# Group norm, attention and projection on one core: how the first chunks of x are loaded and normalised

## The chip, the cores and the metric

One core of a Trainium2 chip runs the whole kernel. The metric is the device time of one execution in microseconds, lower is better. The time before is 1604.12 us, the median of three runs (1601.0 to 1604.14).

## The reference

An attention layer over images. x has 4 images of 512 channels by 48 x 48 = 2304 positions, in float32. Cut to what matters:

```python
xr = x.reshape(b, 32, c // 32, h, w)
mean = xr.mean(axis=(2, 3, 4), keepdims=True)
var = xr.var(axis=(2, 3, 4), keepdims=True)
hn = ((xr - mean) * rsqrt(var + 1e-5)).reshape(b, c, h, w) * scale + bias
qkv = einsum('oc,bchw->bohw', qkv_w, hn) + qkv_b      # then to float16, 8 heads of 64
w = softmax(einsum('bhct,bhcs->bhts', q * s, k * s))
a = einsum('bhts,bhcs->bhct', w, v)
out = x + einsum('oc,bchw->bohw', proj_w, a) + proj_b
```

The normalisation takes one mean and one variance for each group of 16 channels over all positions. As scale and bias of a channel it is x * ga + gb, with rstd = (var + eps)^-0.5, ga = rstd * scale and gb = bias - mean * ga.

## The kernel before, in words

Channels lie on the 128 partitions, so an image is four chunks c of 128 channels, and each chunk is five pieces (blocks) j along the positions: four of 512 and a short one of 256 (`QBLOCKS`). A piece is one tile `hn[b, c, j]`, normalised in place.

The fast path has a prologue for image 0, and then one long stream in which scores, exponentials, values and the projections of later and earlier images are interleaved by a planner (`fill`, `put` and the lists of pieces with their costs and due times). The change touches the prologue alone. What sets its order is the order in which the program is written, since every engine takes its own instructions in order:

- `load_x` (L503) issues the pieces of x. Chunk 0 goes over two DMA queues in turn, pieces 0, 2 and 4 on SP and 1 and 3 on ACT (L537); then ACT issues the weights of k and of q for the first pair of heads (`load_w`), and all other pieces and weights go over SP. A tile's users wait for its load by one of eight DMA semaphores that are taken in turn, so a DMA also waits until the one eight places before it has landed.
- `keep_busy` (L1315) issues filler matmuls on TensorE, 16 ahead of everything and 4 after the first group's small products.
- `stats` and `aggregate` (L617 to L626) take mean and variance of each channel on VectorE: one statistics instruction a piece, then one aggregate into `moments`.
- `first_group` (L670) does chunk 0: the group means come from a tiny product with the matrix `share` (L678), the spread between a group's channels is added to the variance on VectorE (L679, L680), a second tiny product averages that (L681), POOL takes the power -0.5 (L686), and VectorE forms ga and gb (L690, L691).
- `group_scale` and `coefficients` (L632, L652) do the same for chunks 1 to 3 without TensorE: VectorE transposes `moments` in 32 x 32 squares, aggregates over the 16 channels of a group, POOL takes the power, and VectorE spreads the result back to channels. Between the two stand one or two statistics instructions of the next chunk, which fill VectorE while POOL works.
- `norm_chunk` (L701) normalises the five blocks of a chunk on ScalarE with scale ga and bias gb.
- Eight accumulation chains (k for all five blocks, q for the first three) stand in eight PSUM banks at once. The loop over c at the end (L1342) gives each chain the products of chunk c with the first pair's weights (`qk_steps`, L748), one block after another: k of blocks 0, 1, 2, 3, 4, then q of blocks 0, 1, 2. A block of 512 is two pairs of matmuls. TensorE meets each chunk for the first time in the order of those blocks.

After the last chunk the q chains for blocks 3 and 4 and the v chains follow, and then the stream begins.

Of the kernel before, what the change touches and what calls it, by code (L numbers as in the profile page):

```python
# [12 lines left out]
F32 = mybir.dt.float32  # L13
# [3 lines left out]
AF = mybir.ActivationFunctionType  # L17
ALU = mybir.AluOpType
# [6 lines left out]
GROUP = C // 32  # L25
EPS = 1e-5
P = 128
NC = C // P
# [14 lines left out]
QB = 512  # L43
QBLOCKS = [(o, min(QB, T - o)) for o in range(0, T, QB)]
NQ = len(QBLOCKS)
# [422 lines left out]
def fast_path(  # L468
# [12 lines left out]
    nc = tc.nc  # L481
# [11 lines left out]
    ps_s = ctx.enter_context(tc.tile_pool(name="ps_s", bufs=3, space=PSUM))  # L493
    ps_av = ctx.enter_context(tc.tile_pool(name="ps_av", bufs=1, space=PSUM))
# [3 lines left out]
    hn = {}  # L498
# [1 line left out]

    SPARE = {(1, 2): lambda c: ("res", RES), (1, 3): lambda c: (f"a32_{c}", 1)}

    def load_x(b, j, c, engine):  # L503

        o, n = QBLOCKS[j]
        name = f"x_{b}_{c}_{j}"
        if (b, j) in SPARE:
            tag, bufs = SPARE[b, j](c)
            t = work.tile([P, n], F32, tag=tag, bufs=bufs, name=name)
        else:  # L510
            t = xpool.tile([P, n], F32, tag=f"x{c}_{j}", name=name)
        engine.dma_start(t, x[b, bass.ts(c, P), o : o + n])
        hn[b, c, j] = t

    def load_block(b, j):
# [3 lines left out]
    gsc = const.tile([P, NC], F32, name="gsc")  # L519
    gbi = const.tile([P, NC], F32, name="gbi")  # L520
# [13 lines left out]

    for c in range(NC):
        for j in range(NQ):
            load_x(0, j, c, nc.scalar if c == 0 and j % 2 else nc.sync)  # L537
        if c == 0:
            load_w(1, slice(0, P), nc.scalar)
            load_w(0, slice(0, P), nc.scalar)  # L540
# [29 lines left out]
    mhalf = const.tile([P, 2], F32, name="mhalf")  # L570
# [31 lines left out]
    def small_bank(name):  # L602
        return ps_w.tile([P, QB], F32, tag="pw", name=name)


    stat, coef, ab = {}, {}, {}
# [5 lines left out]
    SQ = 32  # L612
    NGROUP = SQ // GROUP
    moments = const.tile([P, 3, SQ], F32, name="moments")
    nc.gpsimd.memset(moments, 1.0)

    def stats(b, j, c):  # L617

        if b not in stat:
            stat[b] = small.tile([P, NC, NQ, 6], F32, tag="st", bufs=1, name=f"st_{b}")  # L620
        nc.vector.bn_stats(stat[b][:, c, j, :], hn[b, c, j])  # L621

    def aggregate(b, chunks=ALL):
        for c in chunks:
            nc.vector.bn_aggr(
                moments[:, 1:, c], stat[b][:, c].rearrange("p j s -> p (j s)")  # L626
            )

    def small_tile(n, tag):
        return small.tile([P, n], F32, tag=tag, bufs=1, name=tag)  # L630
# [21 lines left out]
    def coefficients(b, chunks=ALL):  # L652
        both, spread, rstd = coef.pop((b, chunks[0]))
        nc.vector.tensor_copy(
            spread[:, 1], rstd.unsqueeze(2).to_broadcast((P, NGROUP, GROUP))
        )
        cols = small_tile(SQ * 2, "cols").rearrange("p (s c) -> p s c", s=2)
        nc.vector.transpose(cols, both)
        cs = slice(chunks[0], chunks[-1] + 1)
        ga, mga, gb = (  # L660
            small.tile([P, NC], F32, tag=f"{n}{chunks[0] % 2}", name=f"{n}_{b}")[:, cs]
            for n in ("ga", "mga", "gb")
        )
        nc.vector.tensor_tensor(ga, cols[:, 1, cs], gsc[:, cs], ALU.mult)
        nc.vector.tensor_tensor(mga, cols[:, 0, cs], ga, ALU.mult)
        nc.vector.tensor_tensor(gb, gbi[:, cs], mga, ALU.subtract)
        for i, c in enumerate(chunks):
            ab[b, c] = ga[:, i : i + 1], gb[:, i : i + 1]

    def first_group():  # L670

        mean, var = moments[:, 1, 0:1], moments[:, 2, 0:1]
        by = share.rearrange("p g j -> p (g j)")
        pm = small_bank("first_group")
        dev, var2, mg, veps, rstd = (
            small_tile(1, f"first_{n}") for n in ("dev", "var2", "mg", "veps", "rstd")
        )
        nc.tensor.matmul(pm[:, 0:1], by, mean, start=True, stop=True)  # L678
        nc.vector.tensor_tensor(dev, mean, pm[:, 0:1], ALU.subtract)  # L679
        nc.vector.tensor_scalar(var2, dev, dev, var, ALU.mult, ALU.add)  # L680
        nc.tensor.matmul(pm[:, 1:2], by, var2, start=True, stop=True)  # L681
        nc.vector.scalar_tensor_tensor(
            mg, pm[:, 0:1], -1.0, gsc[:, 0:1], ALU.mult, ALU.mult
        )
        nc.vector.tensor_scalar(veps, pm[:, 1:2], EPS, None, ALU.add)
        nc.gpsimd.tensor_tensor(rstd, veps, mhalf[:, 0:1], ALU.pow)  # L686

        def finish():
            ga, gb = small_tile(1, "first_ga"), small_tile(1, "first_gb")
            nc.vector.tensor_tensor(ga, rstd, gsc[:, 0:1], ALU.mult)  # L690
            nc.vector.tensor_scalar(gb, rstd, mg, gbi[:, 0:1], ALU.mult, ALU.add)  # L691
            ab[0, 0] = ga, gb

        return finish

    def norm(b, j, c):
        t = hn[b, c, j]
        ga, gb = ab[b, c]
        nc.vector.tensor_scalar(t, t, ga, gb, ALU.mult, ALU.add)

    def norm_chunk(b, c):  # L701

        ga, gb = ab[b, c]
        for j in range(NQ):
            t = hn[b, c, j]
            nc.scalar.activation(t, t, AF.Identity, bias=gb, scale=ga)

    def piece(us, run, first=False, last=False, when=None):
        return [us, run, first, last, when, 0, NG]
# [262 lines left out]
    av, acc, pts, avx, sums, rowd, ibs = {}, {}, {}, {}, {}, {}, {}  # L976

    stream = []
    for g in range(NG):
        for j, (o, n) in enumerate(QBLOCKS):  # L980
            count = NT * n // QB // BURST
# [255 lines left out]
    for b in range(B):  # L1237
        g = b * NPAIR
# [71 lines left out]

    busy = ppool.tile([P, 2, QB], F16, tag="p", name="busy")
    nc.vector.memset(busy[:, 0, :], 1.0)
    idle = ps_av.tile([P, QB], F32, tag="av", name="idle")

    def keep_busy(count):  # L1315
        for _ in range(count):
            nc.tensor.matmul(
                idle, busy[:, 0, :P], busy[:, 0, :], start=True, stop=True
            )

    def all_stats(c):
        for j in range(NQ):
            stats(0, j, c)
        aggregate(0, (c,))

    keep_busy(16)
    all_stats(0)
    first_coefficients = first_group()
    keep_busy(4)

    eight = [(1, j) for j in range(NQ)] + [(0, j) for j in range(8 - NQ)]
    banks = [
        t[:, i, :]
        for k in range(3)
# [5 lines left out]
    chains = [qk_steps(0, *a, bank) for a, bank in zip(eight, banks)]  # L1340

    for c in range(NC):  # L1342

        for j in range(NQ):
            if j == (1 if c < 2 else 2):
                if c == 0:
                    first_coefficients()
                else:
                    coefficients(0, (c,))
                norm_chunk(0, c)  # L1350
            if c + 1 < NC:
                stats(0, j, c + 1)
        if c + 1 < NC:
            aggregate(0, (c + 1,))
            group_scale(0, (c + 1,))
        for i, chain in enumerate(chains):
            evacuate = chain(c)
            if c == NC - 1 and i % 2 == 1:

                before()  # L1360
                evacuate()
            before = evacuate
# [68 lines left out]
    for n in range(end):  # L1431
# [29 lines left out]
        if n - BEHIND in soon:  # L1461
            g, j = stream[n - BEHIND][:2]
# [9 lines left out]
    g, b, j = NG - 1, B - 1, NQ - 1  # L1472
    n = QBLOCKS[j][1]
# [42 lines left out]
    o = QBLOCKS[j][0]  # L1516
# [99 lines left out]
```

## Time and profile before

| what | us |
|---|---|
| median of three runs | 1604.12 |
| the runs | 1601.0, 1604.12, 1604.14 |
| the profiled execution | 1602.89 |
| its span, first to last instruction | 1601.2 |
| TensorE busy in the span | 1583.9 |
| first instruction of a real product (L748) | 11.67 after the span's start |

The profile is of one execution. Its times count from the first instruction. TensorE is called PE, VectorE DVE, ScalarE ACT and GpSimd POOL; PEld is the weight load, and a q after the name is an engine's sequencer or queue. Busy times overlap between engines and add up to more than the span. A group's mean duration can be longer than the distance between its instructions, since neighbours overlap: the statistics of 512 elements take 0.68 us each and start every 0.59 us. The line numbers are those of the kernel before.

### The profile page before, as it was taken

The page shows a single profiled execution, that of the slowest core. Times are in us where ns is not written, and L with a number is a line of the kernel's source. Part 1 is how long each engine was busy: PE and PEld are TensorE (multiplying, and loading weights), DVE is VectorE, ACT ScalarE, POOL GpSimd, SP SyncE. Part 2 cuts the span into 40 slices and gives each one's busy share as a digit, 9 for nine tenths or more (in the row PEclk, how much of TensorE's full clock was granted, in tenths as well). Part 3 has the DMA queues.
Part 4 walks back from the last instruction along what each step waited for, and adds up shares of the span by engine and source line. Part 5 has one row for each costly group of instructions (what it writes and reads, how often), then busy time and mean ns, then how long its engine had stood idle before and what let it go on. Part 6 is the DMA issues. An engine that isn't in the chain of part 4 may idle for free.

```text
span 1601.2 us, 28364 instructions
## 1 busy us (share of the span) xinstructions
PE 1583.9 (99%) x11524; PEld 695.0 (43%) x11524; DVE 1137.0 (71%) x1298; ACT 1268.1 (79%) x1362; POOL 327.9 (20%) x460
## 2 busy tenths in 40 slices
PE   9999999999999999999999999999999999999997
PEld 3533434443333534555333354445533334435554
DVE  6177668876666678887666666888767776766775
ACT  3177777888888888888888888877878888888895
POOL 1011212222121222222112111222212121111322
PEclk9999999999999999999999999999999999999999
DMA  7002020000000024521000001353101000015424
GB/s 217 8 14 67 11 71 17 18 15 12 14 18 15 9 70 119 145 64 28 11 15 18 14 12 41 111 154 90 25 15 18 15 15 11 15 31 163 151 67 128
DMA packets 94896, 82.10 MB, mean 51 GB/s; under 512 B 50852, under 2 KB 60964, under 8 KB 94756
## 3 DMA queue, kind: packets, MB, share of 16 engines
q1 hardware_dynamic: 92724, 78.35, 18.1%
q8 instruction: 92, 1.51, 0.4%
q10 hardware_dynamic: 1904, 1.84, 0.4%
q14 instruction: 48, 0.39, 0.1%
q0 software_dynamic: 128, 0.01, 0.0%
HBM read 60.70 MB, written 19.17 MB: 50 GB/s over the span
## 4 chain that ended last, share of the span: by engine, by line
PE 96%; DVE 1%; ACT 1%; DMA 1%; POOL 0%; issue 0%; SPq 0%; DVEq 0%
PE pqk L748 29%; PE ps L998 20%; PE av L1023 20%; PE pv L799 15%; PE pr L887 8%; PE sl L1082 2%; PE ps L748 1%; ACT p L1005 1%; DMA x<-x_dram 0%; DMA r<-x_dram 0%; DVE acc L1054 0%; PE first_av L748 0%; PE first_w L748 0%; DVE st L621 0%; POOL a L879 0%
## 5 line engine op out<-in xcount | busy, mean ns | idle before, releaser
L1005 ACT ACTIVATE p<-ps 128x1024 f16<-128x1024 f32 x1296 | 1233.3, 1025 | 302.5 <-PE ps L998 299.5
L1054 DVE TENSOR_TENSOR acc<-acc,p 128x3072 f16<-128x3072 f16 x270 | 487.2, 1805 | 54.0 <-ACT p L1005 51.6
L748 PE MATMUL pqk<-x,wqkv 128*64 128x512 f32 (+1 forms) x2432 | 510.2, 549 | 0.1
L1023 PE MATMUL av<-p,v 128*64 128x512 f16 (+1 forms) x2880 | 360.8, 364 | 0.4 <-DVE slx L1098 0.3
L998 PE MATMUL ps<-q,k 64*128 64x512 f16 (+1 forms) x2880 | 356.2, 358 | 1.5 <-ACT p L1005 1.1
L799 PE MATMUL pv<-wqkv,x 128*64 128x256 f32 x2304 | 267.5, 379 | 0.0
L748 PEld LDWEIGHTS pqk<-x,wqkv 128*64 128x64 f32 x2432 | 168.0, 137 | 205.9 <-issue 156.2
L1120 POOL TENSOR_SCALAR in<-sums 128x8 f32<-128x8 f32 (+1 forms) x158 | 101.3, 641 | 723.8 <-DMA sums<-slx 717.2
L998 PEld LDWEIGHTS <-k 64*128 64x128 f16 x2880 | 106.0, 94 | 288.5 <-issue 239.6
L1023 PEld LDWEIGHTS <-v 128*64 128x64 f16 x2880 | 131.3, 109 | 213.3 <-issue 168.6
L1147 POOL TENSOR_TENSOR att<-avx,ib 128x512 f16<-128x512 f32 (+1 forms) x78 | 126.5, 1622 | 434.2 <-DMA ib<-row 372.4
L799 PEld LDWEIGHTS pv<-wqkv,x 128*64 128x64 f32 x2304 | 161.7, 137 | 85.4
L1054 DVE TENSOR_TENSOR acc<-p,p 128x3072 f16<-128x3072 f16 x79 | 138.1, 1748 | 0.0
L887 PE MATMUL pr<-a,whi 128*128 128x512 f32 (+1 forms) x311 | 121.9, 399 | 2.6 <-DVE r L914 2.2
L1059 DVE TENSOR_TENSOR acc<-acc 128x1024 f16<-128x1024 f16 x156 | 112.5, 721 | 3.3
L887 PE MATMUL pr<-a,wlo 128*128 128x512 f32 (+1 forms) x311 | 113.6, 373 | 0.0
L758 DVE TENSOR_SCALAR k<-pqk,bqkv 128x512 f16<-128x512 f32 (+1 forms) x75 | 52.1, 695 | 77.4 <-PE pqk L748 77.2
L807 DVE TENSOR_TENSOR v<-pv,bv 128x512 f16<-128x512 f32 x72 | 49.6, 689 | 80.9 <-PE pv L799 80.8
L758 DVE TENSOR_SCALAR q<-pqk,bqkv 128x512 f16<-128x512 f32 (+1 forms) x77 | 53.4, 694 | 74.6 <-PE pqk L748 74.4
L1098 DVE COPY slx<-sl 128x512 f32<-128x512 f32 (+1 forms) x79 | 50.6, 640 | 66.0 <-PE sl L1082 66.0
L914 DVE SCALAR_TENSOR_TENSOR r<-pr,bproj,r 128x512 f32<-128x512 f32 (+1 forms) x80 | 54.9, 694 | 45.3 <-PE pr L887 40.2
L1032 DVE COPY avx<-av 128x512 f32<-128x512 f32 (+1 forms) x79 | 50.6, 640 | 38.5 <-PE av L1023 38.1
(102 smaller groups left out, 498.6 us busy)
## 6 DMA issues: line engine op xcount, KB each, us to landing
r<-x_dram SPq DMA_DIRECT2D x72, 256.0 KB, 3.6
out_dram<-r SPq DMA_DIRECT2D x69, 256.0 KB, 2.7
ib<-row SPq DMA_DIRECT2D x126, 128.0 KB, 3.1
x<-x_dram SPq DMA_DIRECT2D x62, 256.0 KB, 4.1
x<-x_dram SPq DMA_DIRECT2D x16, 128.0 KB, 5.0
sums<-slx SPq DMA_DIRECT2D x128, 2.0 KB, 2.1
ib<-row SPq DMA_DIRECT2D x30, 64.0 KB, 2.9
wqkv<-qkv_wT_dram SPq DMA_DIRECT2D x2, 768.0 KB, 6.9
```

The costliest lines, as they stand in the source:

```text
L748: nc.tensor.matmul(pw[0][lo : lo + D, :n], wqkv[:, c, w0 + lo : w0 + lo + D], hn[b, c, j], start=(c == 0), stop=(c == NC - 1),)
L758: nc.vector.tensor_scalar(qk[g][part][:, o : o + n], pw[0][:, :n], bqkv[:, col : col + 1], SCALE, ALU.add, ALU.mult,)
L799: nc.tensor.matmul(pw[0][lo : lo + D, a, :], hn[b, c, i * P // QB][:, at + lo : at + lo + D], wqkv[:, c, 2 * C + half * C // 2 :][:, : C / ...
L887: nc.tensor.matmul(ps[:, :n], w[:, c, bass.ts(m, P)], at32[b, j, c], start=(i == 0), stop=(i == len(steps) - 1),)
L914: nc.vector.scalar_tensor_tensor(xt[:, i], places[i], bias, xt[:, i], ALU.add, ALU.add)
L998: nc.tensor.matmul(ps[:, h, a * n : (a + 1) * n], kt[rows, bass.ts(i, P)], qt[rows, o : o + n], start=True, stop=True,)
L1005: nc.scalar.activation(pt[:, r], ps, AF.Exp)
L1023: nc.tensor.matmul(av[0][lo : lo + D, :n], vv[b, pr // 2][:, i, pr % 2 * P + lo : pr % 2 * P + lo + D], pt[:, r, h, a * n : (a + 1) * n], ...
L1054: nc.vector.tensor_tensor(t, before, pt, ALU.add)
L1059: nc.vector.tensor_tensor(t[:, 0], t[:, 0], t[:, r], ALU.add)
L1120: nc.gpsimd.tensor_scalar(t, sm, limit, None, op)
L1147: nc.gpsimd.tensor_tensor(atts[g][:, o : o + n], avx.pop((g, j))[:, :n], ibs.pop((g, j))[:, :n], ALU.mult,)
```

## The change

Four things are changed, all in the prologue.

1. Piece 0 of chunk 0 is loaded by two DMAs of 64 channels each, one on SP and one on ACT. ACT's stands ahead of pieces 1 and 3.
2. In every chunk of image 0 the short block (j = 4) is normalised first and comes first in TensorE's order: k of block 4, then of 0, 1, 2, 3, then q of 0, 1, 2.
3. The short block, and in chunk 0 block 0 too, is normalised in two steps. The first multiplies by scale and adds -mean * scale, and needs no variance; it is issued beside POOL's power. The second multiplies by rstd and adds the bias. In chunk 0 VectorE does the second step on the short block and ScalarE on block 0; in the other chunks ScalarE does both steps. The remaining blocks take ga and gb in one step as before.
4. In chunk 0 the group variance is a sum of two products on TensorE (of the channels' variances and of the squared deviations) in place of one product of their sum. In chunks 1 to 3 the mean is spread back to channels by a transpose of its own ahead of the power, and the scale by another after it. The statistics of the next chunk no longer stand between the power and its use, except one ahead of chunk 0's second step; all others of a chunk follow the coefficients of the chunk before.

The diff, cut to its core:

```diff
-    def load_x(b, j, c, engine):
+    def load_x(b, j, c, *engines):
...
-        engine.dma_start(t, x[b, bass.ts(c, P), o : o + n])
+        rows = P // len(engines)
+        for i, engine in enumerate(engines):
+            at = c * P + i * rows
+            engine.dma_start(
+                t[bass.ts(i, rows)], x[b, at : at + rows, o : o + n]
+            )
...
-            load_x(0, j, c, nc.scalar if c == 0 and j % 2 else nc.sync)
+            if c == 0 and j == 0:
+                load_x(0, j, c, nc.sync, nc.scalar)
+            else:
+                load_x(0, j, c, nc.scalar if c == 0 and j % 2 else nc.sync)
...
+    def scale_bias(c, tag, col, mg):
+        ga, gb = (small_tile(1, f"{n}_{tag}") for n in ("ga", "gb"))
+        nc.vector.tensor_tensor(ga, col, gsc[:, c : c + 1], ALU.mult)
+        nc.vector.tensor_scalar(gb, col, mg, gbi[:, c : c + 1], ALU.mult, ALU.add)
+        ab[0, c] = ga, gb
+
+    def shifted(c, tag, mean):
+        mg = small_tile(1, f"mg_{tag}")
+        nc.vector.scalar_tensor_tensor(
+            mg, mean, -1.0, gsc[:, c : c + 1], ALU.mult, ALU.mult
+        )
+        return mg
+
+    def by_scalar(t, scale, bias):
+        nc.scalar.activation(t, t, AF.Identity, bias=bias, scale=scale)
+
+    def by_vector(t, scale, bias):
+        nc.vector.tensor_scalar(t, t, scale, bias, ALU.mult, ALU.add)
...
-        nc.tensor.matmul(pm[:, 0:1], by, mean, start=True, stop=True)
-        nc.vector.tensor_tensor(dev, mean, pm[:, 0:1], ALU.subtract)
-        nc.vector.tensor_scalar(var2, dev, dev, var, ALU.mult, ALU.add)
-        nc.tensor.matmul(pm[:, 1:2], by, var2, start=True, stop=True)
-        nc.vector.scalar_tensor_tensor(
-            mg, pm[:, 0:1], -1.0, gsc[:, 0:1], ALU.mult, ALU.mult
-        )
-        nc.vector.tensor_scalar(veps, pm[:, 1:2], EPS, None, ALU.add)
+        nc.tensor.matmul(pm, by, mean, start=True, stop=True)
+        nc.tensor.matmul(pv, by, var, start=True, stop=False)
+        nc.vector.tensor_tensor(dev, mean, pm, ALU.subtract)
+        nc.vector.tensor_tensor(dev2, dev, dev, ALU.mult)
+        nc.tensor.matmul(pv, by, dev2, start=False, stop=True)
+        mg = shifted(c, "a", pm)
+        small_first, then = hn[0, c, NQ - 1], hn[0, c, 0]
+        by_scalar(small_first, gsc[:, c : c + 1], mg)
+        by_scalar(then, gsc[:, c : c + 1], mg)
+        nc.vector.tensor_scalar(veps, pv, EPS, None, ALU.add)
         nc.gpsimd.tensor_tensor(rstd, veps, mhalf[:, 0:1], ALU.pow)
...
+        meanwhile()
+        by_vector(small_first, rstd, gbi[:, c : c + 1])
+        by_scalar(then, rstd, gbi[:, c : c + 1])
+        scale_bias(c, "a", rstd, mg)
+        for j in range(1, NQ - 1):
+            by_scalar(hn[0, c, j], *ab[0, c])
+
+    def next_group(c):
...
+        nc.vector.tensor_scalar(veps, grouped[:, :, 1], EPS, None, ALU.add)
+        nc.gpsimd.tensor_tensor(rstd, veps, mhalf, ALU.pow)
+        means, mean_cols = small_tile(SQ, "means"), small_tile(SQ, "mean_cols")
+        nc.vector.tensor_copy(by_group(means), to_channels(grouped[:, :, 0]))
+        nc.vector.transpose(mean_cols, means)
+        mg = shifted(c, tag, mean_cols[:, c : c + 1])
+        first = hn[0, c, NQ - 1]
+        by_scalar(first, gsc[:, c : c + 1], mg)
+        scales, cols = small_tile(SQ, "scales"), small_tile(SQ, "cols")
+        nc.vector.tensor_copy(by_group(scales), to_channels(rstd))
+        nc.vector.transpose(cols, scales)
+        by_scalar(first, cols[:, c : c + 1], gbi[:, c : c + 1])
+        scale_bias(c, tag, cols[:, c : c + 1], mg)
+        for j in range(NQ - 1):
+            by_scalar(hn[0, c, j], *ab[0, c])
...
-    keep_busy(16)
-    all_stats(0)
-    first_coefficients = first_group()
-    keep_busy(4)
+    keep_busy(16, ps_av.tile([P, QB], F32, tag="av", name="idle"))
+    for j in range(NQ):
+        stats(0, j, 0)
+    aggregate(0, (0,))
+
+    def meanwhile():
+        keep_busy(4, ps_av.tile([P, QB], F32, tag="av", name="idle_again"))
+        stats(0, 0, 1)
+
+    first_group(meanwhile)
...
-    eight = [(1, j) for j in range(NQ)] + [(0, j) for j in range(8 - NQ)]
+    eight = [(1, j) for j in (NQ - 1, *range(NQ - 1))] + [(0, j) for j in range(8 - NQ)]
...
     for c in range(NC):
-
-        for j in range(NQ):
-            if j == (1 if c < 2 else 2):
-                if c == 0:
-                    first_coefficients()
-                else:
-                    coefficients(0, (c,))
-                norm_chunk(0, c)
-            if c + 1 < NC:
-                stats(0, j, c + 1)
         if c + 1 < NC:
-            aggregate(0, (c + 1,))
-            group_scale(0, (c + 1,))
+            for j in range(NQ):
+                if (j, c) != (0, 0):
+                    stats(0, j, c + 1)
+            next_group(c + 1)
         for i, chain in enumerate(chains):
             evacuate = chain(c)
```

## Prediction

> **What bounds the kernel now.** I read the busy times first, then the table of stages, then the chain of waits over the first 60 us. Of the page's first part one line matters, and of the stage table (length; then busy time and count for PE, PEld, DVE, ACT, POOL; clock; DMA) the first four:
>
> ```profile
> PE 1583.9 (99%) x11524; PEld 695.0 (43%) x11524; DVE 1137.0 (71%) x1298; ACT 1268.1 (79%) x1362; POOL 327.9 (20%) x460
> ```
>
> ```profile
> 0.00:11.67 11.67, 8.12 (x24) 3.02 (x25) 6.09 (x16) 2.15 (x3) 4.42 (x18) 1.00 0.90 274
> 11.67:37.50 25.83, 25.83 (x130) 9.26 (x132) 17.84 (x53) 12.81 (x19) 2.08 (x3) 1.00 0.60 186
> 37.50:60.00 22.50, 22.50 (x196) 13.87 (x194) 4.97 (x8) 0.00 (x0) 0.00 (x0) 1.00 0.15 44
> 60.00:1560.00 1500.00, 1496.32 (x10940) 650.52 (x10937) 1084.23 (x1196) 1230.39 (x1315) 308.99 (x421) 1.00 0.17 45
> ```
>
> From 11.67 us on, TensorE has no idle time before 60 us and 3.68 us in the next 1500. Its useful work begins at 11.67 (the 8.12 us before are filler and two tiny products), so the change, which lies wholly ahead of 37.5 us, is worth what it moves that start, provided TensorE stays fed. The chain of waits (start, length, what) gives the road to 11.67:
>
> ```profile
> 0.80 4.05 DMA x<-x_dram
> ...
> 4.87 2.81 DVE st L621 x5
> ...
> 7.78 0.30 DVE moments L625
> ...
> 9.80 0.59 POOL first_rstd L686
> ...
> 10.80 0.82 ACT x L706
> 11.63 0.04 issue
> 11.67 4.94 PE ps L748 x24
> ```
>
> The timeline of VectorE (start, length) fills in the middle:
>
> ```profile
> 8.55 0.15 DVE L679 TENSOR_TENSOR first_dev<-moments,first_group 128x1 f32<-128x1 f32 x1 [0.47 <-PE first_group L678]
> 8.74 0.27 DVE L680 TENSOR_SCALAR first_var<-first_dev,moments 128x1 f32<-128x1 f32 x1
> 9.49 0.16 DVE L682 SCALAR_TENSOR_TENSOR first_mg<-first_group,gsc 128x1 f32<-128x1 f32 x1 [0.48 <-PE first_group L681]
> 9.56 0.15 DVE L685 TENSOR_SCALAR first_veps<-first_group 128x1 f32<-128x1 f32 x1
> 10.41 0.16 DVE L690 TENSOR_TENSOR first_ga<-first_rstd,gsc 128x1 f32<-128x1 f32 x1
> 10.49 0.27 DVE L691 TENSOR_SCALAR first_gb<-first_rstd,first_mg,gbi 128x1 f32<-128x1 f32 x1
> ```
>
> The reader is to see two hand-overs between VectorE and TensorE ahead of POOL's power, and after it ga, gb, then a whole 128x512 ScalarE pass (0.81 us) before the first product.
>
> [...] the SP and ACT queues move 256 KB each by 4.02 and 4.30 us, side by side. [...] here filler runs from 1.52 to 7.98, again from 9.31 to 10.33, and the first products come at full pace (0.43 us a pair)[...].
>
> **Part 1, the load by two queues.** Piece 0 (256 KB) was the first of SP's; it landed at 4.85. By the packet records the queues carried their first 128 KB by 3.34 (SP) and 3.58 (ACT), and a landing follows the last packet by about 0.73 (4.30 to 5.03). So both halves should be there at 3.58 + 0.73 = 4.3, a gain of 0.55. But ACT's half now stands ahead of pieces 1 and 3 and of the weights for k. Piece 1 was ACT's first 256 KB (landed 5.03); it is now bytes 128 to 384 KB, and that queue reached 384 KB at 5.04: landing 5.77. Piece 2 moves up to 384 KB of SP's queue (4.48, landing 5.2), piece 3 back to 640 KB of ACT's (6.20, landing 6.95), piece 4 up (5.9). The statistics take 0.593 us apiece and 0.41 for the short last one, in the order 0 to 4. Before they ran from 4.87 to 7.67 without a wait. Now after piece 0 they wait for piece 1: 5.79 + 3 x 0.593 + 0.41 = 7.98; by piece 3: 6.97 + 0.593 + 0.41 = 7.97. Part 1 costs 0.31. Bounds: a gain of at most 0.14, since the 16 filler matmuls hold TensorE until 7.98 against a first tiny product at 8.13; a loss of 0.6 if piece 1 lands another 0.3 later.
>
> The same queue holds back more. The k weights (landed 9.1) come 0.2 to 0.6 later, 9.3 to 9.7; they are wanted at 11.1: nothing, with 1.4 us of cover. The q weights' issue now waits on ACT for the landing of ACT's half (semaphore reuse), some 2 us later than 2.2; behind it stand only the table load (1.28 us, done by about 7.2, wanted at 9.3). With 7.3 us to landing, the q weights come at 10.4 to 12.0; they are wanted by the sixth block at 14.9. SP's loads for chunk 2 queue behind those landings (before, the fifth SP load after piece 4 also stood until 9.11), and are read from 16.5 on. All nothing.
>
> **Part 2, the first group.** The variance is formed on TensorE, so VectorE's second step is a plain 0.155 us product in place of 0.272 (L680): 0.12 saved. The mean-times-scale step, which stood ahead of veps after the second product (9.49 to 9.56), is done earlier: 0.08 saved. The third tiny product lies beside VectorE's two steps: nothing. The power starts 0.19 earlier relative to the moments. After it, before: 10.38 to ga 10.41 to gb's end 10.77 to ScalarE 10.80 to 11.62 to TensorE 11.67, 1.29 us. Now: 0.03, then one VectorE pass over 256 elements (L699, later in the program, has 0.482 for this shape), then 0.055 to TensorE: 0.57. Saved 0.72; together 0.91.
>
> Set against the clock with part 1: moments 8.39, first product 8.44, dev 8.86, dev squared 9.06 to 9.21, last tiny product 9.27, veps 9.69 to 9.84, power 9.93 to 10.51, short block done 11.03, TensorE 11.08. The added steps: ScalarE's first step on the short block at 9.33 to 9.92 and on block 0 to 10.63, just over the power, then its second step 10.67 to 11.47. TensorE needs it at 11.08 + 0.43 = 11.51 and may start at 11.52. Block 1 needs gb (VectorE, behind the short block: 11.3) and ScalarE (11.37): ready 12.23, wanted 12.38. Later blocks come every 0.71, wanted every 0.86. One statistics pass (0.68) stands ahead of the power's reader on VectorE as before: covered by the power.
>
> Start 11.67 to 11.08: 0.59 gained; about 0.05 lost after the first block before is not lost again: 0.6.
>
> **Part 3, the other chunks.** Each chunk takes 6.44 us on TensorE, so chunk 1 is wanted at 17.55 (short block) and 17.98. Before: aggregate 12.91, veps ends 14.40, power 15.18, coefficients 16.26. Now four statistics passes from 11.2 end at 13.4; aggregate 13.43, power 15.0 to 15.7, means, their transpose and mg beneath it (15.44), scales 15.73 to 16.17, ScalarE's second step 16.2 to 16.79, ready 16.85: 0.7 ahead; block 0 ready 17.56: 0.4 ahead. The pass that used to fill VectorE's wait for the power is not there, so chunk 2's five statistics run from 16.5 to 19.3 instead of ending at 18.4: ready 22.75, wanted 23.99. Chunk 3 is ready some 6.1 later, wanted 6.44 later. With cover in all three: nothing. If the cover were gone, each microsecond late is a microsecond of TensorE.
>
> **The sum.** The profiled execution took 1602.89 (span 1601.20 and 1.69 around it). The shift passes through to the end, since nothing after 11.67 waits for a clock of its own: 1602.3. The three timed runs have median 1604.12 and lie from 1601.0 to 1604.14, so median and profile differ by twice the gain. From the median the sum gives 1603.5, from the profile 1602.3; I state 1602.9.
>
> **Rivals.**
> A, forecast: start near 11.1, 0.6 gained. Chance 0.55.
> B, part 1 does no harm (piece 1 lands by 5.4): moments at 7.93 to 8.07, the gain is 0.9 to 1.05, about 1602.5. For it: one queue's byte curve is no law for another order. Against: ACT's queue has 128 KB more ahead of piece 1. Chance 0.25.
> C, the change does not do what it says: ScalarE is still busy with block 0's first step, or chunk 1 is late by the 0.4 us of cover, and the gain is eaten: 1603.5. Chance 0.12.
> D, slower: the second queue. Each statistic waits for its piece in order; if piece 1 lands after 5.46 + 0.91 = 6.4 us (0.6 later than I work out), or piece 3 after 7.6, the start is later than 11.67 and the loss grows one for one; at 7.4 it is 1.0, so 1604.0. For it: piece 4's queue slowed to 128 KB in 0.85 us around 5.5; against: both queues together kept some 350 GB/s here. Chance 0.08.
>
> **Numbers.** What a measurement of this kernel can tell from no change is about 0.2%, 3.2 us. None of the cases reaches that: TensorE's whole idle time ahead of 11.67 is 3.55 us. So the chances of faster and slower are those of the runs' own scatter (3.1 us between three runs of one kernel): faster 0.08, within 0.88, slower 0.04. The range takes cases A to D (0.3 to 1.0 either way) and that scatter: 1600.7 to 1604.9.
>
> **What would show it.** Right: the wait before the second statistic of chunk 0 ends on a DMA near 5.8; the moments near 8.4; the first real product near 11.1, of 256 columns; no TensorE idle time from there to 60 us; the power's reader a VectorE pass of 0.48. Wrong: statistics back to back from 4.3 (case B); a wait of TensorE on ScalarE inside chunk 0 or ahead of chunk 1 (C); on a weights' DMA; or a slow pace of the first products, 0.86 a pair, which would be the clock.

## The result, and the profile after

| | before | after |
|---|---|---|
| median of the timed runs | 1602.09 (22 runs, 1600.78 to 1604.55) | 1604.13 (22 runs, 1602.57 to 1605.7) |
| ratio after / before | | 1.0013, interval 1.0007 to 1.0019 |
| the profiled execution, its span | 1602.89, 1601.2 | 1604.05, 1602.2 |
| moments of chunk 0 ready | 8.07 | 9.53 |
| first real product on TensorE | 11.67 | 12.15 |
| products of chunk 0 done | 18.16 | 20.43 |

The changed kernel is slower by 2.0 us, where 0.6 less was forecast. That is below the 0.2% of the forecast's bound, but its interval leaves 1 out.

The busy times are those of before but for a microsecond or two (first part of the page of after):

```profile
PE 1585.3 (99%) x11526; PEld 695.7 (43%) x11526; DVE 1138.5 (71%) x1302; ACT 1270.5 (79%) x1366; POOL 325.9 (20%) x460
```

TensorE's 1.4 us more is hardly more work (two tiny products): it is mainly a stretch at half clock. The stage table of after has it, one column before the last two (length; busy time and count for PE, PEld, DVE, ACT, POOL; clock; DMA share; GB/s):

```profile
5.88:9.29 3.41, 1.39 (x7) 0.42 (x5) 2.36 (x5) 0.91 (x1) 0.00 (x0) 1.00 1.06 327
9.29:12.70 3.41, 2.42 (x14) 1.25 (x14) 2.39 (x10) 2.53 (x5) 0.58 (x1) 1.00 1.07 366
12.70:16.12 3.42, 3.42 (x10) 1.00 (x10) 3.25 (x11) 2.07 (x3) 0.07 (x1) 0.50 1.05 342
16.12:20.43 4.31, 4.31 (x22) 1.40 (x20) 3.88 (x12) 3.72 (x6) 0.64 (x1) 1.00 1.02 359
```

From 12.70 to 16.12 TensorE is busy without a break and does 10 matmuls, where the next 4.31 us at full clock hold 22. The profile of before had a clock of 1.00 in every stage up to 1560 us. The timeline of TensorE shows what came ahead (start, length, line; in brackets the idle time before and what ended it):

```profile
6.67 0.59 PE L1367 MATMUL idle<-busy 128*128 128x512 f16 x2
9.58 0.38 PE L707 MATMUL first_means<-moments,share 128*128 128x1 f32 x2 [2.31 <-DVE moments L633]
9.83 0.36 PE L708 MATMUL first_vars<-moments,share 128*128 128x1 f32 x2
10.41 0.38 PE L711 MATMUL first_vars<-first_dev,share 128*128 128x1 f32 x2 [0.22 <-DVE first_dev L710]
10.65 1.02 PE L1367 MATMUL idle_again<-busy 128*128 128x512 f16 x4
12.15 4.15 PE L799 MATMUL ps<-x,wqkv 128*64 128x256 f32 x12 [0.48 <-DVE x L695]
```

The fillers end at 7.27 and the small products come at 9.58, a gap of 2.31. Before, it was 0.14:

```profile
1.52 6.47 PE L1317 MATMUL idle<-busy 128*128 128x512 f16 x16 [1.52 <-DVE busy L1312]
8.13 0.38 PE L678 MATMUL first_group<-moments,share 128*128 128x1 f32 x2
```

Of the 2.17 us between the two gaps, 1.46 come from the later moments and 0.72 from fillers that ended earlier in this execution. The chain of waits says why the moments are late (start, length, what):

```profile
2.05 6.04 DMA x<-x_dram
8.09 0.02 issue
8.11 1.03 DVE st L629 x2
...
9.24 0.30 DVE moments L633
...
9.58 0.40 PE first_means L707 x2
...
11.07 0.59 POOL first_rstd L717
11.66 0.03 issue
11.69 0.42 DVE x L695
12.11 0.04 issue
12.15 6.73 PE ps L799 x24
```

Before, the chain had piece 0's load and then five statistics in one row. Here it has the load of piece 3, 6.04 us from issue to landing, and only the last two statistics behind it. VectorE's timeline shows two waits for loads, 0.88 us for piece 1 and 0.90 for piece 3:

```profile
4.35 0.69 DVE L629 BATCH_NORM_STATS2 st<-x 128x6 f32<-128x512 f32 x1 [2.89 <-DMA x<-x_dram]
5.92 1.29 DVE L629 BATCH_NORM_STATS2 st<-x 128x6 f32<-128x512 f32 x2 [0.88 <-DMA x<-x_dram]
8.11 1.02 DVE L629 BATCH_NORM_STATS2 st<-x 128x6 f32<-128x512 f32 x2 [0.90 <-DMA x<-x_dram]
```

So the start moved by +0.485, and of the 3.42 us at half clock behind it half is lost, 1.71: together 2.2. The stream, measured at its first score product (73.82 before), runs 2.27 us later than before from 74 us to 1049 us, without change. There the profiled execution of before has a single wait of 2.16 us for a residual's load, which no other profile here has; so the two profiled executions differ less than the medians do, and the shift up to 1049 us is the measure of the change.

### The profile page after: what moved, and what is told of

Read it like the earlier page. It is cut to its first block, busy times and chain, and to the rows that moved or that the text cites. A ratio compares the mean times of both kernels' runs of the same rounds, so it can differ in the third digit from the quotient of the medians.

```text
span 1602.2 us, 28391 instructions
## 1 busy us (share of the span) xinstructions
PE 1585.3 (99%) x11526; PEld 695.7 (43%) x11526; DVE 1138.5 (71%) x1302; ACT 1270.5 (79%) x1366; POOL 325.9 (20%) x460
## 3 DMA queue, kind: packets, MB, share of 16 engines
q10 hardware_dynamic: 1984, 1.97, 0.4%
## 4 chain that ended last, share of the span: by engine, by line
PE 96%; ACT 1%; DVE 1%; DMA 0%; POOL 0%; issue 0%; ACTq 0%; DVEq 0%
PE pqk L799 29%; PE ps L1049 20%; PE av L1074 20%; PE pv L850 15%; PE pr L938 8%; PE sl L1133 2%; PE ps L799 1%; ACT p L1056 1%; DMA x<-x_dram 0%; PE first_av L799 0%; PE first_w L799 0%; DVE acc L1105 0%; POOL a L930 0%; PE held L1133 0%; ACT a L932 0%
```

## The experiments

Each kernel was timed beside the kernel before, whose median was 1601.4 to 1602.1. The ratio behind each time, with its 95% interval in brackets, is the record's; it differs from the quotient of the two medians by up to 0.0005. Moments, landings and clock are those of one profiled execution of each kernel. "Moments" stands for the end of chunk 0's aggregate, "stream" for the first score product. "One queue" means the changed kernel with piece 0 loaded whole by SyncE. The theories at the start: (1) the split load makes the pieces late, and the idle time that follows halves TensorE's clock; rivals: (2) the new order of normalising costs the time; (3) the clock fell by itself. The recorded expectations name ScalarE ACT, SyncE SP and GpSimd POOL.

**One part alone.** e1_one_queue undoes the split and keeps all else:

```diff
-            if c == 0 and j == 0:
-                load_x(0, j, c, nc.sync, nc.scalar)
-            else:
-                load_x(0, j, c, nc.scalar if c == 0 and j % 2 else nc.sync)
+            load_x(0, j, c, nc.scalar if c == 0 and j % 2 else nc.sync)
```

> The changed kernel with piece 0 of chunk 0 loaded by SP alone, as before; all else as changed. Theory L (the load by two queues makes the pieces late, the late start then lets TensorE's clock fall to half): the moments of chunk 0 are back near 8.1 us, the road from the moments to the first real product keeps the 2.63 us of the changed kernel, so TensorE starts near 10.7 us, at full pace, and the stream of scores stands 0.9 to 1.0 us earlier than in the kernel before; the time is some 3.2 us below the changed kernel and 0.9 below the one before. Rival N (the new normalisation in two steps and the new order of blocks lose the time): TensorE starts at 11 or later or shows a slow stretch, and the time stays above the kernel before.

Measured: 1600.7, ratio 0.9993 (0.9985 to 1.0002); moments 7.95, first product 10.58, clock 1.00, stream 0.97 us earlier than before. Its chain has no load in it; the fillers and the first group lead straight to the first product:

```profile
1.52 6.53 PE idle L1364 x16
8.04 0.36 PE first_means L704 x2
...
10.58 5.07 PE ps L796 x24
```

e2_split_only puts the new load_x and the split, nothing else, into the kernel before:

> The kernel before with the load of piece 0 by two queues alone. Theory L: moments near 9.5 us, first real product near 13.1 (9.5 plus the old road of 3.6), a stretch of 3.4 us at half clock, the stream of scores 1.4 + 1.7 = 3.1 us later than before; the time about 3 us above the kernel before. Rival N: moments within 0.4 us of before, no slow stretch, time as before.

Measured: 1605.62, 1.0022 (1.0014 to 1.0031); moments 9.85, first product 13.86, half clock for 6.83 us from 9.43, stream 3.36 us later. The half clock is in its stage table (columns as above):

```profile
9.43:16.26 6.83, 5.30 (x14) 2.13 (x16) 5.13 (x17) 3.27 (x5) 0.58 (x1) 0.50 1.06 376
```

The split is the whole loss, and the other parts are worth about a microsecond in the stream. Rival 2 falls.

**The clock.** e3_filler has 26 fillers ahead in place of 16, e7_filler36 has 36 (`keep_busy(26, ...)`, `keep_busy(36, ...)`). e6_late_moments takes one queue and makes the moments late without touching a DMA:

```diff
     for j in range(NQ):
         stats(0, j, 0)
+    for _ in range(3):
+        stats(0, 0, 0)
     aggregate(0, (0,))
```

> The changed kernel with 26 filler matmuls ahead in place of 16, so that TensorE is busy to about 9.4 us; the load by two queues stays. Theory L with the clock: the first real product stays near 12.2 us, the stretch at half clock is gone, the stream of scores stands about 0.5 us later than before in place of 2.27; the time is 1.7 below the changed kernel. Rival K (the slow first products have another cause than TensorE's idle time, the crowd of transfers for one): the stretch at half pace stays and the time is that of the changed kernel or above.

> The kernel of the first experiment (piece 0 on SP alone, all else as changed) with three more statistics of piece 0 on VectorE ahead of the aggregate, which write again what they wrote before: the moments come 1.8 us later with not one DMA changed, so that TensorE stands idle as long as in the changed kernel. Theory L with the clock: TensorE starts near 12.4 us and a stretch of 3.4 us at half clock follows; the stream stands 0.8 + 1.7 = 2.5 us later than before. Rival K (the clock falls for another cause, such as the crowd of transfers or the 64-channel load): full pace, the stream 0.8 later than before.

> The changed kernel with 36 fillers ahead, since 26 ended at 8.9 us and left TensorE idle for 1.9 us once more. They end at 10.5 to 12.6 us. Theory L with the clock: no stretch at half clock; the stream stands later than before by the late start alone, 0.5 to 2.0 us by where moments and fillers end. Rival K: a stretch of 3.4 us at half clock all the same, 2.2 us or more.

Measured: e3 1603.47, 1.0008 (1.0000 to 1.0016). Piece 3 landed at 9.23 in its profile, the moments came at 10.68, and 1.86 us of idleness stayed: it decided nothing. e6 1605.02, 1.0017 (1.0009 to 1.0025); moments 10.12, and its stage table shows the half clock with the loads of one queue:

```profile
4.58:8.00 3.42, 2.06 (x10) 0.74 (x8) 3.23 (x6) 1.23 (x1) 0.52 (x4) 1.00 1.12 327
8.00:11.41 3.41, 1.01 (x7) 0.87 (x8) 2.33 (x7) 0.41 (x2) 0.00 (x0) 1.00 1.08 363
11.41:14.82 3.41, 3.41 (x12) 1.21 (x12) 3.29 (x9) 3.33 (x6) 0.58 (x1) 0.50 1.06 383
```

e7 1604.07, 1.001 (1.0001 to 1.0019); moments 9.33 and no idle time above 0.5 us ahead of the first product, and with the split loads the clock stays:

```profile
8.68:12.09 3.41, 3.19 (x19) 1.82 (x17) 0.93 (x5) 0.79 (x2) 0.00 (x0) 1.00 1.08 358
12.09:15.50 3.41, 2.93 (x17) 0.97 (x17) 3.12 (x8) 3.33 (x6) 0.58 (x1) 1.00 1.06 384
```

So the half clock went with the idle time, whatever brought it: a gap of 2.31 us in after and of 3.54 in e6 came with a clock of 0.50 behind it, and in e1 and e7, with none above 0.5 between the fillers and the first product, the clock stayed at 1.00. e7 gained nothing, since 36 fillers hold TensorE until 11.30 and the small products behind them: it pays in start (13.60) what it saves in clock.

The timed runs say how often the clock falls, since the mean granted clock of each is on record to three places. In the profiles this mean is 0.9976 to 0.9983 where the clock stays at the start and 0.9956 to 0.9972 where it falls; half of 3.41 us is 0.001 of a run. A run with 0.998 or more is thus one without a fall (an estimate from these profiles; where in a run a fall lies isn't recorded). Such are 1 of 22 runs of after, none of 13 of e2, none of 15 of e6, 5 of 13 of e3, all 12 of e7, 11 of 13 of e1, and 31 of the 41 of before that were timed beside e1 to e4 (157 of 224 beside all experiments). By this estimate the kernel before loses its clock as well in some executions: of those 41 runs the 10 at 0.997 have a median of 1602.80 and the 30 at 0.998 one of 1601.05. A fall without the change, rival 3, is there in that share of before's runs; it doesn't explain what sets the kernels apart.

**What of the split is late.** Three simple readings first. e4_col_halves splits piece 0 by positions, 128 channels by 256, in place of 64 channels by 512. e5_two_on_sp gives both halves of 64 channels to SyncE. e8_small_late issues GpSimd's four small loads after its constants.

```diff
-        rows = P // len(engines)
+        cols = n // len(engines)
...
-            at = c * P + i * rows
+            at = o + i * cols
...
-                t[bass.ts(i, rows)], x[b, at : at + rows, o : o + n]
+                t[:, bass.ts(i, cols)], x[b, bass.ts(c, P), at : at + cols]
```

```diff
-                load_x(0, j, c, nc.sync, nc.scalar)
+                load_x(0, j, c, nc.sync, nc.sync)
```

> The changed kernel with piece 0 split between the same two queues by columns, 128 channels x 256 each, in place of 64 channels x 512. Sub-theory Q (it is the place in ACT's queue: half of piece 0 ahead of pieces 1 and 3): piece 3 is as late as in the changed kernel, near 8.1 us, moments near 9.5. Sub-theory S (it is the shape of 64 partitions, whose issues took 0.59 us where 128 x 512 took 0.40): the issues take 0.4, piece 3 lands near 7, moments near 8.4, first product near 11.1 at full pace, stream 0.6 earlier than before.

> The changed kernel with both 64-channel halves of piece 0 on SP, ACT's queue as in the kernel before. If the place in ACT's queue makes pieces 1 and 3 late (sub-theory Q), they land as before (5.0 and 6.3 us) and only the extra issue on SP shows: moments near 8.3, first product near 10.9, full pace, stream 0.8 earlier than before. If the shape of 64 channels does it (S: issues of 0.59 us), the pieces behind on SP, 2 and 4, come 1 us or more late: moments at 9 or later and a stretch at half clock.

> The changed kernel with POOL's four small loads (scales and biases, 12 KB in all) issued after POOL's memsets, some 2 us later. Sub-theory P (these small loads hold up single DMA engines in the middle of chunk 0, so that its pieces land long after their queue's byte count has passed): pieces 3 and 4 land near 7, moments near 8.4, first product near 11.1. Otherwise pieces 3 and 4 land at 8 or later as in the changed kernel, moments at 9.5 or later.

Measured: e4 1603.23, 1.0008 (1.0000 to 1.0017), moments 9.31; e5 1605.24, 1.0021 (1.0014 to 1.0027), moments 10.81, though ScalarE's queue has what it has in the kernel before; e8 1603.54, 1.0007 (0.9998 to 1.0016), moments 8.89. None brings piece 4 ahead of 7.6. Neither the place on ScalarE's queue nor the shape of the halves is the cause, though each may change the size. e8 is a weak test: GpSimd's first load was issued at 1.97 in place of 1.31, 0.66 later and not some 2. The kernel before has these loads at 1.31 too, so alone they can't make the difference; whether they take part isn't shown. A half of 64 channels as the first of its queue does take 0.58 to 0.60 us to issue, against 0.38 to 0.42 for a whole piece or a half by positions.

e9_tiny_first leaves piece 0 whole on SyncE and puts a 2 KB load of no use first on ScalarE's queue:

```diff
+    tiny = const.tile([16, 32], F32, name="tiny")
+    nc.scalar.dma_start(tiny, x[0, 0:16, 0:32])
```

> The kernel of the first experiment (piece 0 whole, on SP) with one more load ahead on ACT, of 16 rows x 128 bytes into a tile that nobody reads: piece 0 is not split, no bytes to speak of are added, but the turn of the eight DMA semaphores moves on by one, so that SP's load of chunk 1, piece 1 waits for the tiny load (near 3.5 us) and not for piece 1 (5.0), as in the changed kernel; ACT's other loads are issued 0.4 us later. Sub-theory F (more loads in flight beside chunk 0 make its last pieces late): pieces 3 and 4 land at 7.3 or later, moments at 9 or later, a half-clock stretch in most runs. If it is the splitting itself: moments near 8.2, the stream 0.6 to 0.9 earlier than before.

Measured: 1602.87, 1.0008 (1.0001 to 1.0015); moments 8.90, piece 3 at 7.46 and piece 4 at 7.28, half clock from 11.75. Against e1, the 2 KB make the moments 0.95 later, where the split makes them 1.58 later. So it doesn't take many bytes ahead in a queue.

Two readings of that fell. One was that later loads in flight hold the pieces up. In e10_hold (the changed kernel) and e11_cols_hold (e4) the loads of chunk 1 from its piece 1 on are held until the third statistic of chunk 0, by a write of VectorE's to the tile:

```diff
+                if (c, j) == (1, 1):
+                    t = xpool.tile([P, QB], F32, tag="x1_1", name="x_0_1_1")
+                    nc.vector.memset(t[:, 0:1], 0.0)
+                    nc.sync.dma_start(t, x[0, bass.ts(1, P), QB : 2 * QB])
```

> The changed kernel with all of SP's loads from chunk 1, piece 1 on held until VectorE has done the third statistic of chunk 0 (a memset of one column of that tile stands behind it, and the load waits for the memset). Sub-theory F: with less in flight, pieces 3 and 4 land near 7, moments near 8.4, first product near 11.1, the stream 0.6 earlier than before unless chunk 1 now comes late. Sub-theory S (the 64-channel loads themselves are slow): pieces 3 and 4 at 7.5 or later as in the changed kernel, moments above 9.

> The split by columns with the same hold: neither the 64-channel shape nor early loads of chunk 1 are left, only half of piece 0 on ACT's queue ahead of pieces 1 and 3. Sub-theory F: moments at 8.4 or earlier, against 9.3 without the hold. Sub-theory Q (place in ACT's queue): moments near 9.3 as without it.

Measured: e10 1604.5, 1.0016 (1.0008 to 1.0025), moments 10.27; e11 1603.93, 1.001 (1.0004 to 1.0017), moments 10.02. Loads in flight from chunk 1's piece 1 on are not the cause. The other reading was the q weights' load, which ScalarE issued at 3.2 to 4.6 us in most of the late kernels and at 2.2 in the early ones tried until then. e12_q_on_sp (the changed kernel) and e13_tiny_q_on_sp (e9) move it to the end of SyncE's loads of chunk 1; e14_late_q is one queue with that load held (the constant `mhalf` is written ahead of the loads there):

```diff
-            load_w(0, slice(0, P), nc.scalar)
+        if c == 1:
+            load_w(0, slice(0, P), nc.sync)
```

```diff
         if c == 0:
             load_w(1, slice(0, P), nc.scalar)
+            nc.gpsimd.memset(wqkv[:, 0, 0:1], 0.0)
             load_w(0, slice(0, P), nc.scalar)
```

> The changed kernel, with the load of the q weights moved from ScalarE's queue to the end of SyncE's; ScalarE issues only its half of piece 0, piece 1, piece 3 and the k weights. In the kernels whose moments were late, that load was issued on ScalarE at 3.2 to 4.6 us, amid the pieces of chunk 1; in the early ones at 2.2. If that late issue is what delays pieces 3 and 4: they land by about 7.0, moments end at 8.0 to 8.4, first product near 11.0, no slow clock window, about 1601.3 us. If it is not: pieces 3 and 4 still land at 7.5 to 8.5, moments at 8.9 to 9.6, one slow window, about 1603.5 us.

> The kernel with piece 0 whole and a tiny load first on ScalarE's queue (moments 8.90, pieces 3 and 4 at 7.46 and 7.28), now with the load of the q weights moved to the end of SyncE's queue. If the late issue of the q weights on ScalarE is the cause: moments at about 8.0, pieces 3 and 4 by 6.7, about 1600.8 us. If it is not: moments still near 8.9, pieces 3 and 4 after 7.2, about 1602.9 us.

> The changed kernel with piece 0 on SyncE alone (moments 7.95), with the load of the q weights on ScalarE held until about 3.8 us by a small write of GpSimd's. No other load changes. If the late issue of that load in itself delays pieces 3 and 4: they land after 7.3, moments at 8.8 or later, one slow window, about 1603 us. If not: pieces 3 and 4 at 6.1 to 6.6 as with one queue, moments near 8.0, about 1600.7 us, and the cause lies in what comes before 3 us on ScalarE's queue.

Measured: e12 1604.26, 1.0015 (1.0008 to 1.0022), moments 10.39; e13 1603.24, 1.001 (1.0004 to 1.0017), moments 9.17; e14 1600.25, 0.9993 (0.9985 to 1.0002), moments 7.74 with that load issued at 3.90. This reading falls by all three.

What was left: a later start of ScalarE's loads (e15_act_later: one queue, piece 1 held by a write of VectorE's, no load more), one more load in itself (e16_tiny_third: one queue, the 2 KB load behind piece 3), and a small load ahead of the pieces on either queue (e17_tiny_sp: one queue, the 2 KB load first on SyncE).

```diff
+        if (b, c, j) == (0, 0, 1):
+            nc.vector.memset(t[:, 0:1], 0.0)
```

```diff
         if c == 0:
+            tiny = const.tile([16, 32], F32, name="tiny")
+            nc.scalar.dma_start(tiny, x[0, 0:16, 0:32])
             load_w(1, slice(0, P), nc.scalar)
```

```diff
+    nc.sync.dma_start(tiny, x[0, 0:16, 0:32])
```

> The changed kernel with piece 0 on SyncE alone, with piece 1's issue on ScalarE held by a write of VectorE's to one column of its tile, so that all of ScalarE's loads of chunk 1 are issued about 0.4 us later and no load is added. If a later start of ScalarE's queue in itself is what delays pieces 3 and 4: they land after 7.2, moments at 8.8 or later, one slow window, about 1602.9 us. If an additional load ahead of the pieces is needed: pieces 3 and 4 by 7.0, moments at 8.0 to 8.4, about 1600.8 us.

> The changed kernel with piece 0 on SyncE alone, and the small load of 16 channels by 32 positions put between piece 3 and the k weights on ScalarE's queue: a load more than before, but behind the pieces. If any additional load delays the pieces: pieces 3 and 4 after 7.2, moments at 8.8 or later, about 1602.9 us. If the place ahead of the pieces decides: moments near 8.0, first product near 10.6, about 1600.7 us.

> The changed kernel with piece 0 on SyncE alone, and the small load of 16 channels by 32 positions put first on SyncE's queue: SyncE's pieces 0, 2 and 4 are issued 0.45 us later, ScalarE's at their old times. If an additional small load ahead of the pieces delays them whichever queue it is on: pieces 3 and 4 after 7.2 and moments at 8.9 to 9.5, about 1603 us. If it must be ScalarE's queue: piece 4 only its own 0.45 us later (about 7.0), moments at 8.2 to 8.5, no slow window, about 1601.2 us.

Measured: e15 1600.08, 0.9992 (0.9983 to 1.0001), moments 7.35, though ScalarE's first load was issued only 0.16 late in place of 0.4: a weak test, which e17 makes up for, since ScalarE's loads are on time there. e16 1600.0, 0.9992 (0.9983 to 1.0001), moments 7.56. e17 1603.91, 1.0013 (1.0006 to 1.002), moments 10.62. The same 2 KB load, in two places: the chain of e16, with the load behind the pieces, has no DMA in it: its first small product waits for the end of the fillers.

```profile
1.52 6.28 PE idle L1366 x16
7.80 0.21 PE first_means L706 x2
...
9.11 0.59 POOL first_rstd L716
9.72 0.42 DVE x L694
10.15 0.04 issue
10.19 4.20 PE ps L798 x19
```

The chain of e17, with the load ahead, has 6.87 us from the issue of piece 2 at 1.71 to its landing:

```profile
1.71 6.87 DMA x<-x_dram
8.60 1.62 DVE st L628 x3
10.28 0.05 issue
10.32 0.30 DVE moments L632
```

So one small load more, ahead of the pieces, is enough, on either queue: moments at 8.90 in e9 and 10.62 in e17, against 7.56 in e16 and 7.95 in e1. That the split works in the same way, with a half of piece 0 as the load ahead, is argued from what follows and not tested by itself. The DMA view from 3 to 5 us, first of before, then e16, after and e17, shows a sign of it: the packets of all queues take 98 to 103% of the sixteen engines' time in all four, and move less in the last two.

```profile
DMA packets 411, 0.76 MB, mean 381 GB/s; under 512 B 39, under 2 KB 39, under 8 KB 411
```

```profile
DMA packets 452, 0.78 MB, mean 392 GB/s; under 512 B 66, under 2 KB 74, under 8 KB 452
```

```profile
DMA packets 370, 0.60 MB, mean 301 GB/s; under 512 B 77, under 2 KB 77, under 8 KB 370
```

```profile
DMA packets 409, 0.69 MB, mean 344 GB/s; under 512 B 70, under 2 KB 76, under 8 KB 409
```

This sorts all the profiles. The six without such a load (before, e1, e6, e14, e15, e16) move 372 to 398 GB/s in those 2 us, and where no statistic was added their moments come at 7.35 to 8.07. The thirteen with one move 216 to 344 (216 in e12, whose engines were busy for 78% of that time), and the moments come at 8.89 to 10.81.

The rate alone does not explain the delay. By 5 us e17 had moved 0.96 MB and before 0.92, and yet piece 2 landed at 8.58 in e17, where e1 has 5.91. The packet records show what else differs: a load's packets are drawn apart. On ScalarE's queue the k weights stand behind piece 3. In before their first packet began 0.47 us ahead of the end of piece 3's last one, in after 1.67 ahead. It is 0.83 to 2.24 in the eleven kernels with the additional load on that queue, and 0.57 at most in the other eight. Where the load is on SyncE, the spread is there: in e17 the packets of piece 4 run from 5.37 to 8.51, in before from 5.03 to 6.27, while ScalarE's piece 3 comes at 5.01 in e17, earlier than the 6.34 of before. So in the queue with the load ahead part of a piece's packets fell behind, and the piece waited for them: piece 3 landed 0.40 us after its last packet in after, 0.50 in before.

Why stays open. One more difference can be counted: of the packets of 4 bytes, 16 for each of ScalarE's loads up to 14 us in before and after, 29 to 33 lie ahead of 3.5 us in the thirteen (33 in after); in the six it is 15 at most, and 2 or fewer in five (1 in before). They take 9 to 11 ns each on average in every profile, the late ones too, and no run here ties them to the delay.

## Why the prediction was wrong, step by step

**Part 1, the step that failed.** "Part 1 costs 0.31" takes the moments at which a queue had carried so many bytes in before, gives the pieces new places on that curve, and adds 0.73 for the landing.

The first loads did as worked out: halves at 4.25 and 3.69 (forecast 4.3), piece 1 at 5.91 (5.77). The next did not: piece 2 at 6.20 (5.2), piece 3 at 8.09 (6.95), piece 4 at 8.28 (5.9). Piece 3 ended the wait, and the packet records say where its 1.14 us come from. ScalarE's queue had carried 640 KB at 6.49, forecast 6.20: a small part. But the last packet of piece 3 itself ended only at 7.69, when 309 packets of the k weights behind it had begun, and piece 3 landed 0.40 after that packet. In before its last packet ended at 5.84, with 112 of the next load begun, and it landed 0.50 later. So what failed is the reading of a queue's byte count as the end of a load: with a load ahead, part of a piece's packets fell behind while others of its queue went on. SyncE's curve was slower besides (512 KB at 6.88, before 5.20).

The statistics behind piece 3 then cost what was said (8.11 to 9.53), so the term is 1.46 and not 0.31. Both stated bounds failed: the loss was to be 0.6 at most, and the gain 0.14 at most, because the fillers hold TensorE until 7.98; the same 16 fillers ended anywhere from 6.64 to 8.04 in the other profiles. The split alone cost 3.36 us in the stream (e2, ratio 1.0022).

**The clock, the term that was missing.** That the first products come at full pace, 0.43 us a pair, was true of the profiled execution of before, whose longest gap behind the fillers was 1.34 us (some three of ten timed ones seem to have lost clock, by the estimate above). It was carried over to a start for which the moments were to come at 8.39, so the clock was put at nothing. With moments at 9.53 and fillers that ended 0.72 earlier, a gap of 2.31 us opened, and 1.71 us were lost. This sign was named ("a slow pace of the first products, 0.86 a pair, which would be the clock") but had no price and no place in a rival. The price can be worked out in every profile: what the stream is late by is the shift of the first product, plus half of the half-clock time that is left after it (in after the pairs of products start every 0.85 us at half clock and every 0.43 at full). Times are in us.

| kernel | first product, against 11.67 | half of the half-clock time behind it | sum | stream at 74 us |
|---|---|---|---|---|
| after | +0.485 | 1.71 | +2.19 | +2.27 |
| e2_split_only | +2.19 | 1.20 | +3.39 | +3.36 |
| e6_late_moments | +1.25 | 0.95 | +2.20 | +2.17 |
| e7_filler36 | +1.93 | 0 | +1.93 | +2.05 |
| e9_tiny_first | -0.14 | 1.71 | +1.57 | +1.55 |
| e17_tiny_sp | +2.27 | 1.37 | +3.64 | +3.61 |
| e1_one_queue | -1.09 | 0 | -1.09 | -0.97 |
| e16_tiny_third | -1.48 | 0 | -1.48 | -1.35 |

The other ten profiles agree as well, within 0.2 us.

**Rival D** had the mechanism and the point: "piece 3 after 7.6", the start late "one for one". At 8.09 that is 0.49, and the start was late by 0.485. It got 0.08, because the queues' 350 GB/s of before were taken as the rate after, and its price went without the clock.

**Part 2 was right.** From the moments to the first product took 2.63, forecast 2.69, before 3.60: 0.97 saved against 0.91. In e1_one_queue, without the split, it took 2.62.

**Part 3 was right.** After the first product TensorE has no idle time up to 60 us, neither in after nor in e1_one_queue at full clock, so the cover of 0.4 us for chunk 1 held. The k weights came at 10.49 (forecast 9.3 to 9.7), 1.7 ahead of the first product; the q weights at 12.63 (forecast 10.4 to 12.0), wanted at 17.86; ScalarE's table load ended at 9.66 (forecast 7.2), with the first step at 10.46. All three came later than forecast, and none ended a wait.

**The sum's last step was right:** what the start loses passes through to the end. It was made from the wrong start.

A forecast with part 1 at nothing (rival B) would have been that of e1_one_queue: 0.9 to 1.05 gained, 0.97 measured in the stream, 0.7 in the medians.

## What to carry over

Landing times read from one order of loads hold for that order: put a bound of one to three microseconds on them when a small load goes ahead of large ones (piece 3 came 1.14 later than worked out here, piece 4 2.4), and leave the first large piece whole, as far as this kernel tells. A queue's byte count tells when a load is through only while its packets stay together (640 KB at 6.49 here, the last packet of piece 3 at 7.69): look for the load's own last packet. Where a stall is priced ahead of TensorE's first dense stretch, ask whether the gap lowers the clock, and add half of the half-clock time that follows the first product (1.71 us of 3.42 here). One profiled execution can't show how often that happens; the granted clock of the timed runs does. Undo a bundled change part by part: without the split, the rest of this one gave 1600.0 to 1600.7 in four kernels, below both medians, though the interval against before still reaches 1 in each.

## What the runs showed of the hardware

- Short idle gaps of TensorE were enough for a half clock behind them: 1.21 us (e8), 1.37 (e4), 1.46 (e13) and 2.31 (after), with three pairs of tiny products behind them, all were followed by 3.41 us of half clock. In the profile of before gaps of 0.14, 0.56 and 1.34, apart, were not; by the clock of its timed runs they may be in some three of ten (an estimate). What length of gap is enough these runs don't say.
- The half-clock time was 3.41 or 6.83 us, and began up to 5.4 us after the last filler (7.27 to 12.70 in after). In each profile the pace of the fillers doubles once (from 0.43 us apart to 0.21), at a moment that differs from one profile to the next: 4.6 in e6, 5.9 in after, 7.3 in before. In all thirteen profiles with a fall the half clock begins 3.41 or 6.83 us after that moment (4.58 and 11.41 in e6, 5.88 and 12.70 in after). That is one profile of each kernel; whether the same gap lowers the clock in one execution and not in another they don't show.
- 2 KB first in a queue delayed pieces issued up to 1.4 us behind it in that queue by up to 2.7 us: piece 2 landed at 8.58 in e17, 5.91 in e1. The other queue's first pieces came no later: piece 3 at 5.01 in e17, 6.11 in e1.
